# A four-layer graph attention stack on one core: small products on half of the array's columns, edges checked from the 8-bit masks, other durations in the planner

## The chip, the cores and the metric

The kernel runs on one core of a Trainium2 chip. The metric is the device time in microseconds of one execution. Before the change the median of three runs was 3038.52 us (3034.66 to 3041.53). The engines are named as the profile names them: PE (TensorE matmuls), PEld (its weight loads), DVE (VectorE), ACT (ScalarE), POOL (GpSimd) and SP (SyncE, which here only issues transfers).

## The reference, cut to what matters

Sixteen graphs of 1024 nodes with 256 features pass through four attention layers. Every layer normalizes its input, projects it, and adds to it a softmax-weighted sum over the neighbours:

```python
h = jnp.maximum(_layernorm(x, axis=-1), 0.0)
x = x + layer(h, adj)        # four times, each with its own weights
# inside a layer, for every head (4, 4, 4 and 1 heads):
e = leaky_relu(s_src[:, None] + s_dst[None, :], slope)
e = where(adj == 0, -inf, e)
out = softmax(e, axis=-1) @ (h @ W)
```

The adjacency is an int32 matrix of zeros and ones, symmetric here, of 4 MB for each graph. Layer 2 has types of edges in its definition, and after its attention it has a bias, a ReLU, a residual and a normalization over each head.

## The kernel before, in words

Two programs stand in the kernel. `general_path` takes any adjacency; it runs only if a flag `wrong` was set. `fast_path`, which is what the profile shows, assumes edges that are 0 or 1 and values that don't overflow, and checks both while it works: the sums of the edge check land in `sums`, extremes of the softmax totals in `greatest`, and at the end they become `wrong`.

**The main loop.** `fast_path` has 48 units of work in `main`: layers 0 to 2 of 16 graphs, put in an order in which two graphs are under way together. A unit has 4 heads times 8 blocks of 128 source nodes, so 32 tiles, and all units have 1536. A tile goes through three engines. ACT makes `r`, a ReLU over a row of 1024 targets, in one of two wide PSUM buffers (`weigh`). DVE adds a constant, multiplies by the edge mask and writes the numerators `p` to SBUF (`cover`), and with that the wide buffer is free. PE multiplies `p` by the projected features `v` in 16 products of 64 columns by 65 numbers (`gather`): the 128 columns of the array are used as two halves of 64. There are `TILES` = 12 buffers for `p`.

**The preparation of a unit** (`prepare`, with `normal` and `project`). DVE takes statistics (`st`), POOL makes the inverse deviation with a power (`rs<-rs,neg_half`) and normalizes into `hn`, PE transposes `hn` on the full 128 columns, ACT or DVE applies the ReLU (`hT`), PE projects with `wa` on halves of 64 columns, ACT copies to `v`. Then come three small products on PE, once each for a unit, that this change touches. `mx` holds each partition's maxima of the two score vectors; it is transposed (`pp<-ident,mx`), DVE reduces the rows to `top`, and DVE spreads `top` over a small diagonal `diag`. A product of `ones` and `diag` brings the maxima to all partitions (`pp<-diag,ones`). From them DVE and ACT make the exponentials `fac`, and a third product transposes `fac[:, 0]` (`pp<-ident,fac`) to the rows that go to DRAM (`line`) and come back spread over the partitions (`rows`), which `weigh` reads.

**The last layer** has one head. Its numerators are made in halves of 512 (`weigh_some`, `cover`) and multiplied in `last_sums` (`pp<-v_one,p`), spread over later units. `LATE` says how many tiles after its due time its ACT work may fall.

**Masks and edge check.** `load` brings a graph's adjacency as 8-bit numbers to DRAM (`near`, on POOL's queue) and from there transposed to SBUF (`mask`, on SP's queue). `looked_over` reads the same adjacency once more, as int32, in 8 pieces of 512 KB on SP's queue into two buffers `raw`; `look` squares each piece less one half on ACT and writes the sum. The pieces start `LOOK` = 24 tiles after the graph's first unit, and a piece may be fetched only `IDLE` = 6 us after the last but one was looked at.

**The order.** All instructions are put in order ahead of time by a planner. `Plan.cost` gives each instruction a duration and a delay, `Plan.spend` keeps a clock for each engine, and the loop at the end of `fast_path` offers every step that could be next, chooses on every engine the step that is most due among those that could start within `NEAR` = 60 ns of the first, and takes the earliest over the engines. What the planner writes is the fixed order of each engine's queue; on the chip the engines wait for each other by semaphores. All planned instructions are issued from one line of the helper `timed` (L476), so the profile tells them apart by their tiles only.

Of the kernel before, what the change touches and what calls it, by code (L numbers as in the profile page):

```python
# [9 lines left out]
F32 = mybir.dt.float32  # L10
BF16 = mybir.dt.bfloat16
I32 = mybir.dt.int32
I16 = mybir.dt.int16
FP8 = mybir.dt.float8e4
U8 = mybir.dt.uint8
U16 = mybir.dt.uint16
AF = mybir.ActivationFunctionType
# [3 lines left out]
P = 128  # L21
# [347 lines left out]
LEAST = 2.0**-40  # L369
LIVE = 4  # L370
BANKS = 2
TILES = 12
LATE_TILES = 5
LATE = 32
LATE_SUMS = 64
SLACK = 36
FETCH = 15000.0
# [5 lines left out]
LOOK = 24  # L383
IDLE = 6000.0
LANDED = 4000.0
# [22 lines left out]
ACT_LATE = 160.0  # L408
DVE_LATE = 150.0
POOL_LATE = 100.0  # L410
MARK = 20.0


LARGE = ("v_", "x_cur", "mask", "sums", "near", "greatest", "p0", "p1", "p2", "p3", "p4", "p5", "p6", "p7", "p8", "p9", "r_", "po", "pl", "pp", "row", "hT", "raw", "inv")
# [2 lines left out]
class Plan:  # L417
# [19 lines left out]
    def cost(self, engine: str, op: str, a: tuple, k: dict):  # L437
        size = lambda ap: math.prod(ap.shape[1:])
        aps = [v for v in (*a, *k.values()) if hasattr(v, "shape")]
        n = max(size(v) for v in aps)  # L440
        if engine == "PE":
            out, left = a[0], a[1]
            wide = size(left) > 64
            swap = 110.0 if self.mode not in (None, wide) else 0.0
            self.mode = wide
            if op == "transpose":
                return swap + (110.0 if left.dtype == F32 else 56.0), PE_LATE
            if left.dtype != F32:
                return swap + 57.0, PE_LATE
            return swap + max(59.0, size(out) * 0.833 + 3.0), PE_LATE  # L450
        if op == "dma_start":
            total = math.prod(a[0].shape) * mybir.dt.size(a[0].dtype)
            return (600.0 if engine == "POOL" else 60.0), 2200.0 + total / 180.0
        if engine == "ACT":
            return 50.0 + 0.833 * n + (93.0 if "accum_out" in k else 114.0 * sum(size(v) == 1 for v in aps)), ACT_LATE
        if engine == "DVE":
            if op == "reciprocal":
                return 205.0, DVE_LATE
            if op in ("bn_stats", "scalar_tensor_tensor") or n > 64:
                return 70.0 + 1.042 * n + 55.0 * sum(size(v) == 1 for v in aps) + (MARK if n == 512 else 0.0), DVE_LATE  # L460
            return 65.0 + n, DVE_LATE
        if op == "scalar_tensor_tensor":
            return 200.0 + 2.1 * n, POOL_LATE
        if op == "tensor_tensor" and k.get("op", a[-1]) == ALU.pow:
            return 1025.0, POOL_LATE
        return 200.0 + (1.4 if op == "tensor_scalar" else 2.07) * n, POOL_LATE

    def engine(self, eng, name: str):
        plan = self
# [28 lines left out]
def fast_path(  # L498
# [21 lines left out]
    nc = tc.nc  # L520
    ctx.enter_context(tc.manual_schedule())
    plan = Plan()
    pe, act, dve, pool, sp = (
        plan.engine(e, name)
        for e, name in (
            (nc.tensor, "PE"),
            (nc.scalar, "ACT"),
            (nc.vector, "DVE"),
            (nc.gpsimd, "POOL"),
            (nc.sync, "SP"),  # L530
        )
    )
    G, N, F = x.shape
    H, T, HO = a_src_2.shape
    NB = N // P
    KC = F // P
    QUAD = 4
    NQ2 = NB // 2
# [6 lines left out]
    MAXN = max(HEADS)  # L545

    const = ctx.enter_context(tc.tile_pool(name="const", bufs=1))
    ident = const.tile([P, P], F32, name="ident")
    make_identity(nc, ident)
    neg_half = const.tile([P, NB], F32, name="neg_half")  # L550
    nc.vector.memset(neg_half, -0.5)
    ones = const.tile([2 * MAXN, P], F32, name="ones")
    nc.vector.memset(ones, 1.0)

    greatest = const.tile([P, 2, G * LAYERS], F32, name="greatest")

    sums = const.tile([P, G * NB], F32, name="sums")
# [12 lines left out]
    work = ctx.enter_context(tc.tile_pool(name="work", bufs=2))  # L570
    small = ctx.enter_context(tc.tile_pool(name="small", bufs=4))
# [132 lines left out]

    def looked_over(g: "Graph"):

        of = adj[g.b].rearrange("(p r) m -> p (r m)", p=P)
        for k in range(0, N * N // P, N):
            yield "SP", lambda: at_tile[0] >= min(g.until + LOOK, len(tiles)) and (len(looks) < 2 or (looks[-2] is not None and looks[-2] + IDLE))
            raw = work.tile([P, N], I32, name="raw", bufs=2)  # L710
            sp.dma_start(raw, of[:, k : k + N])
            looks.append(None)
            add(g.until + 2 * STEPS, look(raw, len(looks) - 1), plan.now + LANDED)

    def look(raw: bass.AP, k: int):
        yield "ACT", None
        act.activation(raw, raw, AF.Square, bias=-0.5, accum_out=sums[:, k : k + 1])
        looks[k] = plan.now

    looks = []  # L720

    def mask(g: "Graph", j: int):

# [69 lines left out]
    def prepare(u: "Unit"):  # L793

        n, w, layer = u.n, u.w, u.layer
# [12 lines left out]
        v = u.v[:, :, :width].rearrange("p b (h e) -> p b h e", h=n)  # L808
# [20 lines left out]
        for pair in range(NB // 2):  # L829
# [9 lines left out]
            e = Unit()  # L839
            e.u, e.pair, e.turned, e.left = u, pair, False, 2  # L840
            pairs.append(e)
            g = normal(e, rs)
# [1 line left out]

        yield "DVE", lambda: not u.left and u.there
        s, d = (v[:, :, :, w + c].rearrange("p b h -> p h b") for c in range(2))
        mx = small.tile([P, 2, MAXN], F32, name="mx", bufs=3)[:, :, :n]
        dve.tensor_reduce(mx, v[:, :, :, w : w + 2].rearrange("p b h c -> p c h b"), AX.X, ALU.max)
        yield "PE", free_bank
        pm, k = bank()  # L850
        pe.transpose(pm[: 2 * n, :P], mx.rearrange("p c h -> p (c h)"), ident)
        yield "DVE", None
        top = small.tile([2 * MAXN, 1], F32, name="top", bufs=3)
        dve.tensor_reduce(top[: 2 * n], pm[: 2 * n, :P], AX.X, ALU.max)
        drop(k)
        diag = small.tile([2 * MAXN, 2 * MAXN], F32, name="diag", bufs=3)
        dve.tensor_scalar(diag[: 2 * n, : 2 * n], ident[: 2 * n, : 2 * n], top[: 2 * n], None, ALU.mult)
        yield "PE", free_bank
        pa, k = bank()
        pe.matmul(pa[:, : 2 * n], ones[: 2 * n, :], diag[: 2 * n, : 2 * n])  # L860
        yield "DVE", None
        c = small.tile([P, 7, MAXN], F32, name="c", bufs=2)
        S, D, t, c1, c2, b1, b3 = (c[:, i, :n] for i in range(7))
        dve.tensor_copy(c[:, 0:2, :n], pa[:, : 2 * n].rearrange("p (c h) -> p c h", c=2))
        drop(k)
        wide = lambda ap: ap.unsqueeze(2).to_broadcast([P, n, NB])
        arg = small.tile([P, 3, MAXN, NB], F32, name="arg", bufs=3)[:, :, :n, :]
# [30 lines left out]

        add(u.until, others(), plan.now)
        yield "ACT", None  # L900
        act.activation(u.fac[:, 0], arg[:, 0], AF.Exp)
        u.inv = small.tile([P, n, NB], F32, name=f"inv{n}", bufs=3)
        direct = u is main[0] or n == 1 and u.g.b >= G - DIRECT
        if direct:

            yield "PE", free_wide
            pr, k = wide_bank()
            for b in range(NB):
                pe.matmul(pr[:, b * P : (b + 1) * P], u.fac[:, 0, 0, b : b + 1].to_broadcast([P, P]), ident)
            yield "DVE", None  # L910
            over = units.tile([P, N], F32, name="rows", bufs=ROWS)
            dve.tensor_copy(over, pr)
            leave_wide(k)
            u.row.append((over, plan.now))
            if n == 1:
                add(u.until + LATE, last_layer(u), plan.now)
                return
        yield "PE", free_bank
        pr, k = bank()
        pe.transpose(pr[: n * NB, :P], u.fac[:, 0].rearrange("p h b -> p (h b)"), ident)  # L920
        yield "DVE", None
        row = small.tile([MAXN * NB, P], F32, name="row", bufs=1)
        dve.tensor_copy(row[: n * NB], pr[: n * NB, :P])
# [106 lines left out]
    at_tile = [0]  # L1030
# [222 lines left out]
    for b in range(G):  # L1253
        g = Graph()
# [3 lines left out]
        for layer in range(LAYERS):  # L1258
            u = Unit()
# [7 lines left out]
    fresh, live, third = list(layers), [], -3  # L1267
    while fresh or live:
        t = len(main)
        can = [e for e in live if t - e[1] >= 2] or (live if not fresh or len(live) == 2 else [])  # L1270
        pick = None
        for e in can:
            if e[0] == 2 and (t - third >= 3 or not fresh):
                pick = e
        if pick is None:
            pick = max((e for e in can if e[0] < 2), key=lambda e: e[0], default=None)
        if pick is None and fresh and len(live) < 2:
            pick = [0, t, fresh.pop(0)]
            live.append(pick)
        if pick is None:  # L1280
            pick = min(live, key=lambda e: e[1])
        if pick[0] == 2:
            third = t
        main.append(pick[2][pick[0]])
        pick[:2] = [pick[0] + 1, t]
        live = [e for e in live if e[0] < 3]

    if G > 5:

        b = G - 4  # L1290
# [3 lines left out]
    STEPS = H * NB  # L1294
    turn = {(u.g.b, u.layer): k * STEPS for k, u in enumerate(main)}
    begins = []
    for b, us in enumerate(layers):
        us[0].g.until = turn[b, 0] - LOADED
        begins.append((turn[b, 0] - EARLY, load(us[0].g), us[0].g.until))
        for k, u in enumerate(us):  # L1300

            u.past = us[k - 1] if k else None
            if u.n > 1:
                at = turn[b, k] // STEPS
# [20 lines left out]
    def add(until, gen, ready, first=None):  # L1325
        jobs.append([until, ready, *(first or next(gen))[:2], gen])

    tiles = [(u, h, j) for u in main for h in range(H) for j in range(NB)]
    while True:
# [3 lines left out]
        can = []  # L1333
# [9 lines left out]
        if at_tile[0] < len(tiles) and r_ready is not False:  # L1343
            u, h, j = tiles[at_tile[0]]
# [3 lines left out]
        if whole[0] < WHOLES and sum(t is not None for t in p_free) > SPARE:  # L1348
            k = next(
                (  # L1350
                    k
                    for k in range(at_tile[0] + LEAD, min(at_tile[0] + LEAD + NB, len(tiles)))
                    if k not in ahead and tiles[k][2] < NB - LAST
                ),
                None,
            )
            if k is not None:
                u, h, j = tiles[k]
# [10 lines left out]
        for job in jobs:  # L1369
            ready = job[3] is None or job[3]()  # L1370
            if ready:
                ready = max(job[1], ready)
                engine = job[2]
# [7 lines left out]
        for e in ("SP", "POOL", "DVE", "ACT", "PE"):  # L1381
            mine = [c for c in can if c[2] == e]
# [87 lines left out]
```

## Time and profile before

| | before |
|---|---|
| median of three runs | 3038.52 us |
| profiled execution, time | 3040.28 us |
| profiled execution, span | 3038.4 us |
| mean granted TensorE clock | 0.975 |
| PE / PEld busy | 2747.2 / 2257.4 us |
| DVE busy | 2649.5 us |
| ACT busy | 2420.4 us |
| POOL busy | 1572.1 us |
| bytes moved by DMA | 254.02 MB |

The span runs from the first to the last instruction; the profiled execution's time is 1.9 us longer, which is what lies around the span. "Busy" is time in which at least one instruction of an engine is under way. Matmuls overlap each other and their ends are modelled, so PE's busy time is more than what the array needs. A group row of the page gives busy time and the mean duration of one instruction, and then the idle time of its engine just before these instructions with what ended most of it. PE has two records for each fp32 product, so 24,576 products of a `po` tile are 49,152 records.

### The profile page before, as it was taken

What the parts mean: (1) busy time and instruction counts of PE and PEld (TensorE: products, weight loads), DVE (VectorE), ACT (ScalarE), POOL (GpSimd) and SP (SyncE); (2) the same over time, 40 slices, a digit from 0 to 9 for tenths busy, and PEclk for the clock granted to TensorE, in tenths of its full rate; (3) what the DMA queues carried; (4) which work ended last, traced back from release to release, by engine and by line L of the source; (5) the groups of instructions that cost most, each with busy time, mean ns of one, the idle gap of its engine ahead of it and who ended that gap; (6) DMA issues with size and microseconds to landing.
All of it is one profiled execution on the core that took longest, in us unless ns stands there. A gap on an engine that the chain in (4) does not pass through costs nothing.

```text
span 3038.4 us, 129952 instructions
## 1 busy us (share of the span) xinstructions
PE 2747.2 (90%) x58660; PEld 2257.4 (74%) x58660; DVE 2649.5 (87%) x4062; ACT 2420.4 (80%) x3201; POOL 1572.1 (52%) x2263
## 2 busy tenths in 40 slices
PE   6888999899999999899999999999999899989867
PEld 5777777777787777777777777777777777777745
DVE  6889998898989889888988889989898898899973
ACT  5887889778788797878878788787888888888651
POOL 3445673544746547265564646647265473373540
PEclk8999999999999999999999999999999999999979
DMA  8613413325142332414234142422414233311100
GB/s 152 159 68 77 116 38 92 95 67 125 47 109 80 78 106 67 115 61 96 91 73 117 44 102 90 89 92 70 107 68 94 81 84 102 119 43 49 41 8 30
DMA packets 162725, 254.02 MB, mean 84 GB/s; under 512 B 82808, under 2 KB 118384, under 8 KB 161136
## 3 DMA queue, kind: packets, MB, share of 16 engines
q1 hardware_dynamic: 160112, 228.83, 25.3%
q0 software_dynamic: 2048, 16.78, 5.5%
q8 instruction: 462, 7.57, 1.0%
q14 instruction: 103, 0.84, 0.1%
HBM read 261.49 MB, written 34.40 MB: 97 GB/s over the span
## 4 chain that ended last, share of the span: by engine, by line
PE 42%; DVE 27%; ACT 20%; issue 5%; POOL 5%; DMA 0%; ACTq 0%; SPq 0%; DVEq 0%; POOLq 0%
PE pp L476 21%; PE po L476 20%; DVE p L476 17%; ACT r L476 15%; DVE st L476 3%; POOL rs L476 2%; DVE att L476 2%; ACT hT L476 1%; ACT att L476 1%; ACT raw L476 1%; ACT v L476 1%; POOL hn L476 1%; POOL att L476 1%; DVE s L476 1%; DVE c L476 1%
## 5 line engine op out<-in xcount | busy, mean ns | idle before, releaser
L476 ACT ACTIVATE r<-rows,fac 128x1024 f32<-128x1024 f32 (+1 forms) x1552 | 1772.2, 1152 | 349.5 <-DVE p L476 327.1
L476 PE MATMUL po<-v,p 128*64 128x65 f32 x49216 | 1680.7, 226 | 186.3 <-DVE p L476 100.2
L476 PEld LDWEIGHTS po<-v,p 128*64 128x64 f32 x49216 | 1592.9, 140 | 338.1 <-DVE p L476 135.2
L476 DVE SCALAR_TENSOR_TENSOR p<-r,mask 128x1024 f32<-128x1024 f32 x1024 | 1221.7, 1217 | 136.3 <-ACT r L476 112.6
L476 DVE SCALAR_TENSOR_TENSOR p<-r,fac,mask 128x1024 f32<-128x1024 f32 (+1 forms) x768 | 819.4, 1099 | 80.5 <-ACT r L476 71.7
L476 PE MATMUL pp<-wa,hT 128*64 128x264 f32 (+1 forms) x4056 | 520.0, 390 | 21.9 <-ACT hT L476 15.6
L476 POOL TENSOR_TENSOR att<-att,inv 128x512 f32<-128x512 f32 x128 | 133.8, 1045 | 714.1 <-DVE inv L476 576.7
L476 PE MATMUL pp<-v_one,p 128*64 128x257 f32 x3584 | 442.7, 385 | 0.8 <-DVE p L476 0.4
L476 PEld LDWEIGHTS pp<-wa,hT 128*64 128x64 f32 x4056 | 263.2, 138 | 154.3 <-ACT hT L476 25.1
L476 PEld LDWEIGHTS pp<-v_one,p 128*64 128x64 f32 x3584 | 250.3, 139 | 101.4 <-issue 4.4
L476 POOL TENSOR_SCALAR hn<-x_cur,rs 128x256 f32<-128x256 f32 x512 | 283.7, 567 | 44.7 <-PE pp L476 34.6
L476 PE MATMUL pp<-ident,hn 128*128 128x128 f32 x1020 | 182.6, 299 | 57.3 <-POOL hn L476 43.6
L476 POOL TENSOR_TENSOR x_cur<-att,x_cur 128x512 f32<-128x512 f32 x190 | 225.9, 1189 | 14.9
L476 ACT ACTIVATE r<-rows_one,fac 128x512 f32<-128x512 f32 x240 | 185.7, 782 | 20.0 <-DVE p L476 9.6
L476 PEld LDWEIGHTS pp<-ident,hn 128*128 128x128 f32 x1020 | 111.0, 146 | 118.1 <-POOL hn L476 82.4
L476 ACT ACTIVATE hT<-pp 128x512 f32<-128x512 f32 x255 | 150.7, 597 | 42.9 <-PE pp L476 41.2
L476 DVE BATCH_NORM_STATS2 st<-x_cur 128x6 f32<-128x256 f32 x512 | 179.5, 412 | 3.5 <-DMA x_cur<-in_x_dram 3.3
L476 ACT COPY v<-pp 128x264 f32<-128x264 f32 (+1 forms) x395 | 147.2, 386 | 37.4 <-PE pp L476 36.5
L476 POOL TENSOR_TENSOR v<-v,fac 128x512 f32<-128x512 f32 x128 | 137.8, 1097 | 42.4 <-ACT fac L476 42.4
L476 ACT ACTIVATE raw<-raw 128x1024 int32<-128x1024 int32 x128 | 135.0, 1058 | 0.6 <-DMA raw<-in_adj_dram 0.6
L476 POOL TENSOR_TENSOR att<-att,s 128x512 f32<-128x512 f32 x124 | 129.5, 1044 | 10.0
L476 POOL TENSOR_TENSOR rs<-st 128x8 f32<-128x8 f32 x192 | 38.6, 215 | 176.1 <-DVE st L476 174.3
(91 smaller groups left out, 1592.2 us busy)
## 6 DMA issues: line engine op xcount, KB each, us to landing
rows<-line SPq DMA_DIRECT2D x191, 512.0 KB
raw<-in_adj_dram SPq DMA_DIRECT2D x128, 512.0 KB
x_cur<-in_x_dram SPq DMA_DIRECT2D x32, 512.0 KB
near<-in_adj_dram POOLq DMA_DIRECT2D x64, 256.0 KB, 9.0
out_dram<-y SPq DMA_DIRECT2D x128, 128.0 KB
rows_one<-line SPq DMA_DIRECT2D x15, 512.0 KB
mask<-near SPq DMA_TRANSPOSE x64
wa<-in_L_gnn_W_dram SPq DMA_DIRECT2D x6, 128.0 KB
```

What stands on the lines that cost most here:

```text
L476: r = call(*a, **k)
```

## The change

Five things change.

1. The three small products become ordinary products on 64 columns. The inputs lie in one of three zeroed tiles `wide`, with 64 columns for the exponentials, 64 for `mx`, and 8 for `diag`. The transposes become products with the identity, the product with `ones` becomes two, one for each half of the output partitions. The direct route of a few units still uses 128 columns.
2. `looked_over` no longer fetches the adjacency a second time. It reads the 8-bit mask tile of the graph, 8 pieces of 1024 numbers, on ACT, as soon as the masks are loaded, without spacing.
3. `Plan.cost` gets other durations, among them 1650 in place of 1025 ns for POOL's power, 400 in place of 60 ns for an SP transfer, and 1041 in place of 996 ns for a look.
4. `TILES` goes from 12 to 13.
5. `LATE` goes from 32 to 48. `LANES` names a constant that was written as 2 and stays 2.

```diff
-TILES = 12
+TILES = 13
-LATE = 32
+LATE = 48
...
-            return (600.0 if engine == "POOL" else 60.0), 2200.0 + total / 180.0
+            return (600.0 if engine == "POOL" else 400.0), 2200.0 + total / 180.0
+        given = sum(size(v) == 1 for v in aps)
         if engine == "ACT":
-            return 50.0 + 0.833 * n + (93.0 if "accum_out" in k else 114.0 * sum(size(v) == 1 for v in aps)), ACT_LATE
+            if n == 1024:
+                return (1041.0 if "accum_out" in k else (903.0, 1050.0, 1143.0)[given]), ACT_LATE
+            if n <= 64:
+                return 100.0 + 0.7 * n, ACT_LATE
+            return 50.0 + 0.833 * n + 114.0 * given + (40.0 if given == 2 else 0.0), ACT_LATE
...
         if op == "tensor_tensor" and k.get("op", a[-1]) == ALU.pow:
-            return 1025.0, POOL_LATE
-        return 200.0 + (1.4 if op == "tensor_scalar" else 2.07) * n, POOL_LATE
+            return 1650.0, POOL_LATE
+        if op == "tensor_scalar":
+            return (205.0 + 1.3 * n if n > 64 else 270.0), POOL_LATE
+        if n <= 16:
+            return 165.0, POOL_LATE
+        return (1110.0 if n == 512 else 200.0 + 2.07 * n if n > 512 else 200.0 + n), POOL_LATE
...
-    ones = const.tile([2 * MAXN, P], F32, name="ones")
+    ones = const.tile([P, P // 2], F32, name="ones")
     nc.vector.memset(ones, 1.0)
+    wide_of = [const.tile([P, 2 * P // 2 + 2 * MAXN], F32, name=f"wide{k}") for k in range(3)]
+    for t in wide_of:
+        nc.vector.memset(t, 0.0)
...
     def looked_over(g: "Graph"):
-        of = adj[g.b].rearrange("(p r) m -> p (r m)", p=P)
-        for k in range(0, N * N // P, N):
-            yield "SP", lambda: at_tile[0] >= min(g.until + LOOK, len(tiles)) and (len(looks) < 2 or (looks[-2] is not None and looks[-2] + IDLE))
-            raw = work.tile([P, N], I32, name="raw", bufs=2)
-            sp.dma_start(raw, of[:, k : k + N])
-            looks.append(None)
-            add(g.until + 2 * STEPS, look(raw, len(looks) - 1), plan.now + LANDED)
-
-    def look(raw: bass.AP, k: int):
-        yield "ACT", None
-        act.activation(raw, raw, AF.Square, bias=-0.5, accum_out=sums[:, k : k + 1])
+        e = g.edges.bitcast(FP8)
+        for k in range(2 * NQ2):
+            yield "ACT", lambda: max(g.loaded, 1.0)
+            seen = work.tile([P, N], BF16, name="seen", bufs=1)
+            at = g.b * NB + k
+            of = e[:, k // 2, (k % 2) * N : (k % 2 + 1) * N]
+            act.activation(seen, of, AF.Square, bias=-0.5, accum_out=sums[:, at : at + 1])
...
-        mx = small.tile([P, 2, MAXN], F32, name="mx", bufs=3)[:, :, :n]
+        mine = wide_of[turns_of[0] % len(wide_of)]
+        turns_of[0] += 1
+        diag = mine[:, P:]
+        mine = mine[:, :P].rearrange("p (c m) -> p c m", c=2)
+        mx = mine[:, 1, : 2 * n].rearrange("p (c h) -> p c h", c=2)
...
-        pe.transpose(pm[: 2 * n, :P], mx.rearrange("p c h -> p (c h)"), ident)
+        pe.matmul(pm[: P // 2, :P], mine[:, 1, :], ident)
...
-        diag = small.tile([2 * MAXN, 2 * MAXN], F32, name="diag", bufs=3)
...
-        pe.matmul(pa[:, : 2 * n], ones[: 2 * n, :], diag[: 2 * n, : 2 * n])
+        for half in range(0, P, P // 2):
+            pe.matmul(pa[half : half + P // 2, : 2 * n], ones, diag[:, : 2 * n])
...
-        act.activation(u.fac[:, 0], arg[:, 0], AF.Exp)
+        near_end = mine[:, 0, : n * NB].rearrange("p (h b) -> p h b", h=n)
+        act.activation(near_end, arg[:, 0], AF.Exp)
...
-        pe.transpose(pr[: n * NB, :P], u.fac[:, 0].rearrange("p h b -> p (h b)"), ident)
+        pe.matmul(pr[: P // 2, :P], mine[:, 0, :], ident)
```

More of the change, by code (lines that the diff above doesn't have):

```diff
@@ L410 @@
 POOL_LATE = 100.0
-MARK = 20.0
+LANES = 2
 LARGE = ("v_", "x_cur", "mask", "sums", "near", "greatest", "p0", "p1", "p2", "p3", "p4", "p5", "p6", "p7", "p8", "p9", "r_", "po", "pl", "pp", "row", "hT", "raw", "inv")
@@ L452, in cost @@
             total = math.prod(a[0].shape) * mybir.dt.size(a[0].dtype)
-            return (600.0 if engine == "POOL" else 60.0), 2200.0 + total / 180.0
+            return (600.0 if engine == "POOL" else 400.0), 2200.0 + total / 180.0
+        given = sum(size(v) == 1 for v in aps)
         if engine == "ACT":
-            return 50.0 + 0.833 * n + (93.0 if "accum_out" in k else 114.0 * sum(size(v) == 1 for v in aps)), ACT_LATE
+            if n == 1024:
[3 more added lines that the diff above has]
+            return 50.0 + 0.833 * n + 114.0 * given + (40.0 if given == 2 else 0.0), ACT_LATE
         if engine == "DVE":
             if op == "reciprocal":
[L458 to L463, printed above, removed]
-        if op == "tensor_tensor" and k.get("op", a[-1]) == ALU.pow:
-            return 1025.0, POOL_LATE
-        return 200.0 + (1.4 if op == "tensor_scalar" else 2.07) * n, POOL_LATE
+                return 200.0, DVE_LATE
+            if op == "bn_stats":
+                return 327.0, DVE_LATE
+            if op == "scalar_tensor_tensor" and n == 512 and not given:
+                return 716.0, DVE_LATE
+            if op == "scalar_tensor_tensor" and n > 64 or n > 64:
+                return 73.0 + 1.042 * n + 52.0 * given, DVE_LATE
+            return 90.0 + n, DVE_LATE
+        if op == "tensor_tensor" and k.get("op", a[-1]) == ALU.pow:
+            return 1650.0, POOL_LATE
[4 more added lines that the diff above has]
+        return (1110.0 if n == 512 else 200.0 + 2.07 * n if n > 512 else 200.0 + n), POOL_LATE
     def engine(self, eng, name: str):
@@ L551, in fast_path @@
     nc.vector.memset(neg_half, -0.5)
-    ones = const.tile([2 * MAXN, P], F32, name="ones")
+    ones = const.tile([P, P // 2], F32, name="ones")
     nc.vector.memset(ones, 1.0)
+    wide_of = [const.tile([P, 2 * P // 2 + 2 * MAXN], F32, name=f"wide{k}") for k in range(3)]
+    for t in wide_of:
+        nc.vector.memset(t, 0.0)
+    turns_of = [0]
     greatest = const.tile([P, 2, G * LAYERS], F32, name="greatest")
@@ L705, in looked_over @@
     def looked_over(g: "Graph"):
-        of = adj[g.b].rearrange("(p r) m -> p (r m)", p=P)
-        for k in range(0, N * N // P, N):
-            yield "SP", lambda: at_tile[0] >= min(g.until + LOOK, len(tiles)) and (len(looks) < 2 or (looks[-2] is not None and looks[-2] + IDLE))
-            raw = work.tile([P, N], I32, name="raw", bufs=2)
-            sp.dma_start(raw, of[:, k : k + N])
-            looks.append(None)
-            add(g.until + 2 * STEPS, look(raw, len(looks) - 1), plan.now + LANDED)
-    def look(raw: bass.AP, k: int):
-        yield "ACT", None
-        act.activation(raw, raw, AF.Square, bias=-0.5, accum_out=sums[:, k : k + 1])
-        looks[k] = plan.now
-    looks = []
+        e = g.edges.bitcast(FP8)
[5 more added lines that the diff above has]
+            act.activation(seen, of, AF.Square, bias=-0.5, accum_out=sums[:, at : at + 1])
     def mask(g: "Graph", j: int):
@@ L908, in prepare @@
             for b in range(NB):
-                pe.matmul(pr[:, b * P : (b + 1) * P], u.fac[:, 0, 0, b : b + 1].to_broadcast([P, P]), ident)
+                pe.matmul(pr[:, b * P : (b + 1) * P], near_end[:, 0, b : b + 1].to_broadcast([P, P]), ident)
             yield "DVE", None
@@ L1269, in fast_path @@
         t = len(main)
-        can = [e for e in live if t - e[1] >= 2] or (live if not fresh or len(live) == 2 else [])
+        can = [e for e in live if t - e[1] >= LANES] or (live if not fresh or len(live) == LANES else [])
         pick = None
@@ L1276, in fast_path @@
             pick = max((e for e in can if e[0] < 2), key=lambda e: e[0], default=None)
-        if pick is None and fresh and len(live) < 2:
+        if pick is None and fresh and len(live) < LANES:
             pick = [0, t, fresh.pop(0)]
```

## The prediction, made before the changed kernel ran

> **What bounds the kernel now.** I read the page from the top: busy shares, then the chain of work that ended last, then the groups of instructions.
>
> ```profile
> PE 2747.2 (90%) x58660; PEld 2257.4 (74%) x58660; DVE 2649.5 (87%) x4062; ACT 2420.4 (80%) x3201; POOL 1572.1 (52%) x2263
> PE 42%; DVE 27%; ACT 20%; issue 5%; POOL 5%; DMA 0%; ACTq 0%; SPq 0%; DVEq 0%; POOLq 0%
> PE pp L476 21%; PE po L476 20%; DVE p L476 17%; ACT r L476 15%; DVE st L476 3%; POOL rs L476 2%; DVE att L476 2%; ACT hT L476 1%; ACT att L476 1%; ACT raw L476 1%; ACT v L476 1%; POOL hn L476 1%; POOL att L476 1%; DVE s L476 1%; DVE c L476 1%
> L476 ACT ACTIVATE r<-rows,fac 128x1024 f32<-128x1024 f32 (+1 forms) x1552 | 1772.2, 1152 | 349.5 <-DVE p L476 327.1
> L476 DVE SCALAR_TENSOR_TENSOR p<-r,mask 128x1024 f32<-128x1024 f32 x1024 | 1221.7, 1217 | 136.3 <-ACT r L476 112.6
> ```
>
> No engine is full and no transfer is on the chain. PE, DVE and ACT hand it to each other, PE holding most: 42% of the span. A microsecond taken from PE is worth between 0.42 (only where PE was on the chain) and 1 (if the planner's order follows PE everywhere).
>
> The waits say what the two wide buffers do: ACT waits for DVE to free one, DVE for ACT to fill one, and PE for `hn`.
>
> ```profile
> ACT r L476 <- DVE p L476: 336.7, 477, 6.2
> DVE p L476 <- ACT r L476: 184.2, 306, 4.0
> PE pp L476 <- POOL hn L476: 43.6, 26, 16.3
> ```
>
> **What the Trainium skill says.** "TensorEngine Tiling (Array Packing)", Key Properties: changing the tiling mode, not just the tile, drains the engine; its Restrictions rule out fp32 transpose mode with column tiling, which is why the change multiplies by the identity. "TensorE: Matmul & The Clock Gate", part 3, adds that products on different column groups run side by side. Both agree with the timeline of PE. These are one transposition of `mx`, one product with `diag` and one transposition of `fac`, each on 128 columns inside a run of `po` on 64:
>
> ```profile
> 1259.79 1.40 PE L476 MATMUL po<-v,p 128*64 128x65 f32 x42
> 1261.12 0.27 PE L476 MATMUL pp<-ident,mx 128*8 128x128 f32 x1
> 1261.32 2.09 PE L476 MATMUL po<-v,p 128*64 128x65 f32 x64
> 1263.34 0.38 PE L476 MATMUL pp<-diag,ones 8*128 8x8 f32 x2
> 1263.65 0.97 PE L476 MATMUL po<-v,p 128*64 128x65 f32 x21
> ...
> 1317.78 1.75 PE L476 MATMUL po<-v,p 128*64 128x65 f32 x54
> 1319.46 0.28 PE L476 MATMUL pp<-ident,fac 128*32 128x128 f32 x1
> 1319.67 1.04 PE L476 MATMUL po<-v,p 128*64 128x65 f32 x28
> ```
>
> Another stretch gives the undisturbed pace:
>
> ```profile
> 1004.25 3.65 PE L476 MATMUL pp<-v_one,p 128*64 128x257 f32 x32
> 1007.73 6.70 PE L476 MATMUL po<-v,p 128*64 128x65 f32 x224
> ```
>
> A record of `po` takes 6.70/224 = 29.9 ns. So 42 records fill 1.26 of the 1.53 us from 1259.79 to 1261.32, and `mx` took the other 0.27; in the same way `diag` took 2.33 - 64 x 0.0299 = 0.42 and `fac` 1.89 - 54 x 0.0299 = 0.28. These are prices with the switch to the other mode and back.
>
> "ScalarE: Activation LUTs", What ACT_TABLE_LOAD costs, gives an activation one element a cycle, fp32 and bf16 alike. The trace agrees for int32: looks follow each other at 0.95 us plus 0.09 for the read of the sum. No run here shows 8-bit input.
>
> **The change part by part.**
>
> *Small products.* In the order of the two programs PE changes between 64 and 128 columns 775 times before and 399 times after; what stays are the transpositions of `hn`. A unit's three products cost 0.27 + 0.42 + 0.28 = 0.97 us. After: in the row of `v_one`, 32 records take 3.48 us, so two products side by side (4 records) 435 ns for 257 columns. A product alone keeps its half that long: 128 columns 435 x 128/257 = 217 ns, twice in a unit. The two products with `diag` have 8 columns and no row like them; I take the price of a pair of `po`, 120 ns. Together 0.55 us, saving 0.41 us, in 64 preparations (48 units and 16 last layers) 26 us of PE. Ends: 40 if the lone product runs wholly beside its neighbours, 10 if it holds up both halves. On the chain this is worth 26 x 0.42 = 11 to 26 us; I take 17.
>
> *Power priced 1650 instead of 1025 ns.* The row by form says the new price is the chip's:
>
> ```profile
> L476 POOL TENSOR_TENSOR rs<-rs,neg_half 128x8 f32<-128x8 f32 x64 | 106.0, 1657 | 5.0
> ```
>
> In 64 preparations the planner was 0.63 us early, 40 us in all, close to the 43.6 us PE stands still for `hn`, with tile products queued behind the transpositions and everybody behind those. With the right price other products go first. Worth 0 to 44; I take 12, since what is put first can itself be late. The other new prices move single instructions by under 60 ns, except SP's 400 for 60, which makes the planner expect rows 0.3 us later. SP issues only.
>
> *Looks.* 128 looks stay on ACT and cost the same, taken from the int32 row. Their places change. Between tiles the order before has 72 single looks and 28 pairs; after, 102 singles, 7 pairs, 2 triples and, in the first unit, one run of six. During a run DVE has at most one finished `r`, 1.14 us of work (its instructions follow each other so), so a pair (2.08 us) leaves it dry for 0.94, a triple 1.98, six 5.1. Before 28 x 0.94 = 26 us, after 6.6 + 4.0 + 5.1 = 16. Gain 11, on the chain 3 to 11; I take 6. If 8-bit input took twice as long, 122 us more on ACT at its 20% of the chain would be 24 us lost; that goes into the range. `seen` has one buffer, so a look right after another waits out its write, 0.1 us (1.05 long against 0.95 apart), some 26 times at most.
>
> *Transfers.* 128 pieces of 512 KB, 67 MB of 254, and their issues on SP go; `rows`, `line` and `out` no longer queue behind them. Of the waits on ACT hardly any is theirs:
>
> ```profile
> L476 ACT ACTIVATE raw<-raw x128: 1040/1050/1137, 73.8 to 2667.4; 128x1024 int32<-128x1024 int32 x128
> ...
>   DMA raw<-in_adj_dram: 0.6, 1
> ```
>
> The chain in order of time has one stretch of 5.4 us behind such a transfer (at 2539). Worth 0 to 8; I take 2.
>
> *Thirteenth buffer.* DVE waits for PE to free a `p` for 7.1 us in all: 0 to 7, I take 1. *`LATE`.* The last layer's PE products per unit go from runs such as 32, 96, 0 to 16, 64, 48: more even, costed at nothing, -5 to +5. *Three zeroed tiles* are memsets like the one of `ones` (0.17 us) while DVE waits 3.3 us for the first input: nothing.
>
> Sum: 17 + 12 + 6 + 2 + 1 = 38 us. The profiled execution took 3040.3 us (span 3038.4 and 1.9 around it), the median is 1.8 lower: 3038.5 - 38 = about 3001.
>
> **The rivals.**
>
> *No gain.* PE's time is freed, but it only stands longer waiting for `p`, because DVE and ACT keep each other's pace through two buffers (336.7 and 184.2 us). For it: in undisturbed stretches a tile costs DVE 1.14 us and PE 0.96 (32 records). Against: PE holds 42% of the chain. Then only a few microseconds remain: 3035.
>
> *Slower, by looks.* They now start as soon as the masks are there, with no spacing. If the gaps on ACT in which the planner puts them are not there on the chip, each delays `r`, and through it DVE and PE. Now `ACT raw` is 1% of the chain, some 30 us. The sum of gains without looks is 32, so it decides from (30 + 32)/1.04 = 60 of 128 looks on the chain. With 90 there it is 94 - 62 = 32 us slower, 3070. Against: the runs got shorter.
>
> *It doesn't do what it says.* Lone products on half of the columns might drain PE as before, for instance with the full-width `ident` as the other operand. Then 17 of the 38 are lost: 3018.
>
> **How the numbers follow.** Likeliest, as summed: 0.66, own range 2972 to 3028 (the low and the high ends of the parts do not fall together). No drain saved: 0.10, at 3018. No gain: 0.11, at 3035. Slower by looks or by an order that fits worse: 0.13, at 3070. A measurement of this kernel tells 0.2%, 6 us, from no change: faster is below 3032.4, and takes the first two cases and a little of the third, 0.78; same 0.09; slower 0.13. Eight times in ten: 2965 to 3042.
>
> **What would show it.** In the profile after: PE rows `pp<-ident,wide` and `pp<-wide,ones` on 64 columns, no step of 0.15 to 0.2 us at their edges, and PE's busy time down by some 20 us; `PE pp <- POOL hn` below 30 us; `ACT raw` gone and `ACT seen` at most 1% of the chain, 1.04 us each; 187 MB moved. The prediction is wrong if `DVE p <- ACT r` grows by tens of us, or if PE's idle time grows by what its work shrank.

## The result and the profile after

The changed kernel took 3015.2 us (median of four runs, 3013.71 to 3019.46), against 3039.7 us before (with a fourth run added to the three): a ratio of 0.9924, interval 0.9907 to 0.9941, so about 24 us or 0.8% faster. The forecast was 3001 us with a range of 2965 to 3042. The direction and the range held, though the range of 77 us held the kernel before as well; the gain is about two thirds of the 38 us of the sum. The profiled execution took 3014.4 us, its span 3012.4.

First the engines' busy time and the chain that ended last, by engine and by line:

```profile
PE 2694.6 (89%) x58915; PEld 2262.8 (75%) x58915; DVE 2650.3 (88%) x4065; ACT 2414.9 (80%) x3201; POOL 1571.0 (52%) x2263
PE 35%; DVE 29%; ACT 21%; POOL 7%; issue 5%; DMA 1%; SPq 0%; ACTq 0%; POOLq 0%; DVEq 0%
DVE p L487 19%; PE pp L487 19%; PE po L487 16%; ACT r L487 15%; DVE st L487 3%; POOL att L487 2%; ACT seen L487 2%; DVE att L487 2%; ACT att L487 1%; DVE s L487 1%; DVE c L487 1%; POOL rs L487 1%; POOL hn L487 1%; ACT v L487 1%; ACT hT L487 1%
```

PE's busy time is down by 53 us and its share of the chain by seven points, while DVE and ACT do the same work as before and hold a little more of the chain. The span is only 26 us shorter: PE's idle time (span less busy time) went from 291 to 318 us, so half of what its work shrank went into waiting. The prediction had named idle time that grows by as much as the work shrank as a sign of being wrong; half of that came. Then the waits that answer to the three shown before, in us in total, times, and the longest:

```profile
ACT r L487 <- DVE p L487: 349.2, 454, 5.9
DVE p L487 <- ACT r L487: 157.8, 264, 5.7
...
PE pp L487 <- POOL hn L487: 51.8, 32, 15.3
```

DVE waits for ACT 26 us less. PE's wait for `hn`, which was to fall below 30 us, rose from 43.6 to 51.8. The DMA engines moved 186.91 MB, as forecast. The timeline of PE shows what a small product costs now, inside a run of `po`:

```profile
975.98 1.15 PE L487 MATMUL po<-v,p 128*64 128x65 f32 x32
976.98 0.38 PE L487 MATMUL pp<-ident,wide 128*64 128x128 f32 x2
977.11 1.18 PE L487 MATMUL po<-v,p 128*64 128x65 f32 x32
```

```profile
263.23 1.15 PE L487 MATMUL po<-v,p 128*64 128x65 f32 x32 [0.47 <-ACT att L487]
264.22 0.24 PE L487 MATMUL pp<-wide,ones 128*64 128x8 f32 x4
264.31 1.89 PE L487 MATMUL po<-v,p 128*64 128x65 f32 x58
```

At the prediction's pace of 29.9 ns a record, 32 records of `po` fill 0.96 us. From 975.98 to 977.11 are 1.13 us, so the product with `wide` took 0.17; from 263.23 to 264.31 are 1.08, so the two with `ones` took 0.12. That pace is a little high, since it counts the run-out of the last record. The next line of the same stretch shows the 224 records from 1007.73 to 1014.26, which is 29.2 ns each:

```profile
1014.26 3.65 PE L476 MATMUL pp<-v_one,p 128*64 128x257 f32 x32
```

The merged lines also hide that the second pair of `po` after a product on 128 columns still starts 0.05 us late. The starts of the single records give the whole delay that a product hands to the `po` records behind it. The median over all places inside an unbroken run of `po` (40 to 91 of each kind), at 29.2 ns a record, was 0.35 us for `mx`, 0.46 for `diag` and 0.36 for `fac` before, and now 0.19 for each product with `wide` and 0.12 for the two with `ones`. The step from the last `po` to the product is 0.06 us in the stretch at 975.98, where it was 0.15 before, and the one from the product's last record to the next `po` is 0.03, where it was 0.20. "TensorEngine Tiling (Array Packing)" of the Trainium skill calls this drain a property of changing the mode, in Key Properties; the traces put it at 1.18 - 0.49 = 0.69 us for a unit's three products, 44 us for 64 preparations if all stand in such runs. The sum had taken 0.41 and 26.

The looks, by tile, with minimum, median and maximum in ns:

```profile
L487 ACT ACTIVATE seen<-mask x128: 1039/1046/1118, 38.1 to 2561.7; 128x1024 bf16<-128x1024 fp8e4 x128
```

8-bit input costs ACT what int32 did (median 1050), so the cost kept for the range didn't come.

### The profile page after: what moved, and what is told of

It is laid out like the page before. It is cut to its first block, busy times and chain, and to the rows that moved or that the text cites. A ratio compares the mean times of both kernels' runs of the same rounds, so it can differ in the third digit from the quotient of the medians.

```text
span 3012.4 us, 130240 instructions
## 1 busy us (share of the span) xinstructions
PE 2694.6 (89%) x58915; PEld 2262.8 (75%) x58915; DVE 2650.3 (88%) x4065; ACT 2414.9 (80%) x3201; POOL 1571.0 (52%) x2263
## 2 busy tenths in 40 slices
DMA packets 144292, 186.91 MB, mean 62 GB/s; under 512 B 80760, under 2 KB 116336, under 8 KB 142704
## 4 chain that ended last, share of the span: by engine, by line
PE 35%; DVE 29%; ACT 21%; POOL 7%; issue 5%; DMA 1%; SPq 0%; ACTq 0%; POOLq 0%; DVEq 0%
DVE p L487 19%; PE pp L487 19%; PE po L487 16%; ACT r L487 15%; DVE st L487 3%; POOL att L487 2%; ACT seen L487 2%; DVE att L487 2%; ACT att L487 1%; DVE s L487 1%; DVE c L487 1%; POOL rs L487 1%; POOL hn L487 1%; ACT v L487 1%; ACT hT L487 1%
## 5 line engine op out<-in xcount | busy, mean ns | idle before, releaser
L487 PE MATMUL pp<-v_one,p 128*64 128x257 f32 x3584 | 430.7, 383 | 2.7 <-DVE p L487 1.8
L487 PEld LDWEIGHTS pp<-wa,hT 128*64 128x64 f32 x4056 | 269.3, 138 | 138.9 <-ACT hT L487 16.5
L487 PEld LDWEIGHTS pp<-v_one,p 128*64 128x64 f32 x3584 | 267.2, 138 | 95.2 <-DVE p L487 9.0
L487 PE MATMUL pp<-ident,hn 128*128 128x128 f32 x1020 | 178.8, 295 | 63.5 <-POOL hn L487 51.8
L487 ACT ACTIVATE seen<-mask 128x1024 bf16<-128x1024 fp8e4 x128 | 134.6, 1052 | 0.4
```

The source lines that it names most:

```text
L487: r = call(*a, **k)
```

## The experiments

All orders are made ahead, so almost any edit gives another order of all instructions, and the time of one order is in part chance, as the nudges at the end show. I therefore separated what an edit does on the chip from what the new order does. Ratios are to the kernel before, timed beside each kernel. Single executions of one kernel spread over some 6 to 20 us, so medians and intervals count, and a single profiled span does not.

| run | what it is | median us | ratio, interval |
|---|---|---|---|
| e1 | before, looks from masks | 3037.7 | 0.9991 (0.9983 to 1.0000) |
| e2 | e1, products on 64 columns, order of e1 | 3027.8 | 0.9964 (0.9952 to 0.9977) |
| e3 | changed, products on the full array, order kept | 3032.7 | 0.9976 (0.9968 to 0.9984) |
| e4 | changed, old prices | 3011.0 | 0.9909 (0.9894 to 0.9924) |
| e5 | e2, products priced as they are | 3034.1 | 0.9985 (0.9977 to 0.9993) |
| e6 | e5 with TILES 13 (e4 with LATE 32) | 3012.6 | 0.9907 (0.9890 to 0.9924) |
| e7 | changed, LATE 32 | 3015.8 | 0.9923 (0.9909 to 0.9936) |
| e8 | changed, planner nudged by 2 ns | 3035.6 | 0.9988 (0.9980 to 0.9995) |
| e9 | e5's order with 13 buffers | 3030.2 | 0.9973 (0.9961 to 0.9984) |
| e10 | before, nudge that changed no order | 3039.7 | 1.0003 (0.9993 to 1.0012) |
| e11 | changed, another nudge | 3007.2 | 0.9894 (0.9874 to 0.9913) |
| e12 | e4, nudged | 3019.4 | 0.9935 (0.9915 to 0.9955) |

**The looks alone (e1).** `looked_over` of the changed kernel in the kernel before, nothing else.

```diff
-            raw = work.tile([P, N], I32, name="raw", bufs=2)
-            sp.dma_start(raw, of[:, k : k + N])
...
+            of = e[:, k // 2, (k % 2) * N : (k % 2 + 1) * N]
+            act.activation(seen, of, AF.Square, bias=-0.5, accum_out=sums[:, at : at + 1])
```

> The kernel before with one part of the change: the edge check reads the 8-bit masks on ACT as they are loaded, so 128 transfers of 512 KB are gone; products, prices, TILES and LATE as before, and the planner makes a new order of it. Theory of the prediction: looks and transfers are worth 8 us (3 to 21), so about 3032 us. Rival, the transfers carry the change: most of its 24.5 us are here, 3020 us or less. Rival, any new order moves the time by chance: anywhere from 3025 to 3055.

A gain of 0.09%, 2.7 us (0 to 5 by the interval). Leaving out 67 MB of transfers, for which ACT had waited 0.6 us in the trace before, bought next to nothing; the gain that the rival expects is not seen. But e1 is a new order too, a single draw, and its looks are not spread as in the changed kernel: between tiles its trace has 94 single looks, 4 pairs, 4 triples, 2 runs of four and one of six. By the prediction's own count they leave DVE dry for 23 us, against 26 before and 16 in the changed kernel. So e1 does not test the better spread.

**The small products at a fixed order (e2, e3).** In e2 the products are on 64 columns, but the planner is given the old price of each, so all engines' orders are those of e1 except for the products themselves:

```diff
+        plan.priced = (False, 110.0)
-        pe.transpose(pm[: 2 * n, :P], mx.rearrange("p c h -> p (c h)"), ident)
+        pe.matmul(pm[: P // 2, :P], mine[:, 1, :], ident)
...
-        pe.matmul(pa[:, : 2 * n], ones[: 2 * n, :], diag[: 2 * n, : 2 * n])
+        for half in range(0, P, P // 2):
+            plan.priced = (True, 0.0 if half else 59.0)
+            pe.matmul(pa[half : half + P // 2, : 2 * n], ones, diag[:, : 2 * n])
```

> The kernel of e1 with the three small products on 64 columns, but priced by the planner as they were, so that every engine's order is that of e1. What moves is the mode change alone. Theory: 17 us below e1 (11 to 26), PE busy down by some 26 us. Rival, PE only waits longer for p: within 5 us of e1, and PE's wait for DVE p up by some 20 us.

The reverse was done to the changed kernel, again with the order kept:

```diff
+        plan.priced = (False, 109.624)
-        pe.matmul(pm[: P // 2, :P], mine[:, 1, :], ident)
+        pe.transpose(pm[: 2 * n, :P], mine[:, 1, : 2 * n], ident)
...
-        for half in range(0, P, P // 2):
-            pe.matmul(pa[half : half + P // 2, : 2 * n], ones, diag[:, : 2 * n])
+        plan.priced = (False, 118.0)
+        pe.matmul(pa[:, : 2 * n], ones[: 2 * n, :], diag[: 2 * n, : 2 * n])
...
+        plan.priced = (False, 109.624)
-        pe.matmul(pr[: P // 2, :P], mine[:, 0, :], ident)
+        pe.transpose(pr[: n * NB, :P], mine[:, 0, : n * NB], ident)
```

> The changed kernel with the three small products back on the full array (8, 32 and 128 columns, as before), priced as the narrow ones, so that every engine's order is that of the changed kernel. Theory: the mode changes cost 17 us here too (11 to 26), about 3032 us. Rival, PE is no longer what bounds (35% of the chain): under 8 us, 3016 to 3023 us.

By the ratios the narrow products are worth 0.9991 - 0.9964 = 0.0027, 8 us, in the order of e1, and 0.9976 - 0.9924 = 0.0052, 16 us, in that of the changed kernel (9.9 and 17.5 us by the medians). In both pairs the intervals are apart. The order was the same in each pair (the traces show it), and so was the mean granted clock of the runs (0.977 in both, 0.974 in both), so this is what the narrow form of the products does on the chip. The first gain lies below the 11 to 26 us of the theory, the second inside. In the changed order the rival of under 8 us falls; in that of e1 the rival of under 5 us is unlikely but not excluded, since the intervals leave anything from 0.0006 to 0.0048. The longer wait that this rival names is not seen: PE's `po` products waited for `p` as before (105.2 us in e1, 105.8 in e2). In the page of e3 PE holds more of the chain than in the changed kernel:

```profile
PE 44%; DVE 26%; ACT 18%; POOL 6%; issue 5%; DMA 1%; SPq 0%; ACTq 0%; POOLq 0%; DVEq 0%
```

That share is no measure of the drains by itself, since it moves with the order: e8 and e6, with narrow products, show 42% and 43%, e11, the fastest, 40%, and e2 31%. Of PE's time only a part came out at the end. Of the 44 us, which hold if every product stands in an unbroken run, it is 0.19 in the order of e1 and 0.36 in that of the changed kernel; of what PE's busy time differs by in the single profiles (19 us from e1 to e2, 41 from e3 to the changed kernel) it is 0.44 and 0.39.

**The prices (e4, e12).** The changed kernel with the whole of the old `Plan.cost`; the power's price stands for the others here.

```diff
-            return 1650.0, POOL_LATE
+            return 1025.0, POOL_LATE
```

> The changed kernel with the old Plan.cost, all else as changed; the order is made anew. Theory of the prediction: the right price of POOL's power is worth 12 us (0 to 44), so about 3027 us. Rival: since PE's wait for hn did not shrink in the changed kernel (51.8 us after 43.6), the prices are worth nothing by themselves: 3010 to 3020 us. Rival, chance of the order: anywhere from 3000 to 3035 us.

It is not slower: 0.9909 against 0.9924, with intervals that overlap. Two more pairs among the runs below differ in the prices alone: e6 against e7, 0.9907 and 0.9923, and e12, which nudges e4, against e8, 0.9935 and 0.9988. In all three the old prices have the lower ratio, by 5, 5 and 16 us, and only in the last are the intervals apart. The price of the power was not changed by itself in any run.

> The kernel of e4 (all of the change but the prices) with the planner's delay after a PE instruction at 212 instead of 210 ns. Theory, the prices are worth nothing and each order is a draw: 3005 to 3035 us. If orders by the old prices are robust, within 5 of 3011 us; if it is below 3005 it is the best kernel of the study.

**From e2 to e4 in steps (e5, e6, e7).** Between 3027.8 and 3011.0 us lie the products' own price, `TILES` and `LATE`.

e5 is e2 without its lines of given prices:

```diff
-        plan.priced = (False, 110.0)
...
-            plan.priced = (True, 0.0 if half else 59.0)
```

> The kernel of e2 (looks from the masks, products on 64 columns, TILES 12, LATE 32, old prices), but with the products priced as what they are now, so that the planner makes its own order. First of three steps from e2 (3027.8 us) to e4 (3011.0 us). Theory: the planner's order gains from knowing that the array does not change its mode, some 5 us: 3023 us. Rival, TILES and LATE make the step: 3028 us within 4. Rival, chance of the order: anywhere from 3015 to 3040.

e6 is e5 with one buffer more:

```diff
-TILES = 12
+TILES = 13
```

> As e5, with TILES 13 and LATE still 32, which is e4 with LATE 32. Second step. Theory of the prediction: a thirteenth buffer is worth 1 us (0 to 7), so within 4 of e5. Rival, the buffer lets ACT and DVE run ahead of PE, and the 17 us are here: 3011 us within 4.

e7 is the changed kernel with the old `LATE`:

```diff
-LATE = 48
+LATE = 32
```

> The changed kernel with LATE 32, all else as changed. Theory of the prediction: LATE is worth nothing, -5 to 5 us: 3010 to 3020. Rival, the later due time of the last layer spreads PE's work and gives the rest of the gain: 3025 or more.

Each of these steps compares two orders, so it holds the chance of an order too. The own price costs 6 us instead of gaining 5. `LATE` shows nothing, in both places (e7 against the changed kernel, e6 against e4). The step to `TILES` = 13 is 0.9985 to 0.9907, 24 us, by far the largest. e9 asks whether that is the buffer: 13 buffers on the chip, taken in turn, in the order that the planner made for 12.

```diff
+    held, idle = {}, list(range(TILES + 1))
...
-        return probs.tile([P, N], F32, name=f"p{k}"), k
+        held[k] = idle.pop(0)
+        return probs.tile([P, N], F32, name=f"p{held[k]}"), k
...
+            idle.append(held[k])
```

> The kernel of e5 with 13 buffers for p on the chip, but the planner still counting 12, so that every engine's order is that of e5; the next buffer is the one longest free. It tells whether the 21 us between e5 (3034.1) and e6 (3012.6) are the buffer or the order made with it. Theory, the order: 3034 us within 4, since DVE waits for a free p for under 15 us in any trace. Rival, the buffer: 3013 to 3020 us.

0.9985 becomes 0.9973: 4 us (-2 to 10 by the intervals, which overlap). So the smaller part of the 24 us, if any, is the buffer under the old order; the rest came with the order made for 13 buffers. DVE's wait for PE to free a `p` did not shrink either: 4.9 us in e5, 8.2 in e9, 12.3 in e6. (It was 21.2 us in e4, over the 15 us that the expectation gives for any trace.) The order made for 13 was not run on 12 buffers.

**Nudges (e8, e10, e11).** A planner's delay moved by 2 ns means nothing to the chip, and the work stays the same to the last instruction.

In e8, e10 and e12 it is the first of these lines, in e11 the second.

```diff
-PE_LATE = 210.0
+PE_LATE = 212.0
...
-DVE_LATE = 150.0
+DVE_LATE = 152.0
```

> The changed kernel with the planner's delay after a PE instruction at 212 instead of 210 ns, a change without meaning on the chip that only makes another order. It measures what an order is worth by chance. If orders of one quality differ little, 3015 us within 4; if the steps of e1 to e7 are partly chance, some 8 us or more away, either side.

> The changed kernel with the planner's delay after a DVE instruction at 152 instead of 150 ns: a third order of the changed work, beside 3015.2 and the 3035.6 of e8. Theory, e8 was an unlucky transient in the first 640 tiles and not the level: 3010 to 3030. Rival, the changed kernel's own order is the lucky one and 3035 the level: 3030 to 3040.

> The kernel before with the planner's delay after a PE instruction at 212 instead of 210 ns, nothing else: another order of the same work. Theory, orders of the same work lie up to 20 us apart: more than 6 us away from 3039, on either side. Rival, only the changed kernel's order was a lucky one: 3039 us within 6.

e10 failed as an experiment: the nudge left the order of every engine as it was. It serves as a control, and its 1.0003 says how well two measurements of one order agree. How far nudged orders of the kernel before would lie apart stays unknown. e8 and e11 did change the order, and the same work took 3035.6 and 3007.2 us: one nudge gave back nearly the whole gain, the other added 8 us to it and fell below both of its forecasts. With e12 against e4 (3019.4 and 3011.0) there are three pairs of nudged orders, 8, 8 and 20 us apart.

Where they part is seen by counting tiles. The order of e8 parts from that of the changed kernel 0.33 ms into the span, the one of e11 at 0.76 ms. These rows count the ACT instructions that read `rows` in two stages of equal length for each kernel (start and end of the stage, its length, busy time of ACT with the count, granted clock, DMA). First the changed kernel, then e8, then e11:

```profile
480.00:1200.00 720.00, 0.00 (x0) 429.69 (x378) 0.99 0.26 64
1200.00:2540.00 1340.00, 0.00 (x0) 808.66 (x710) 0.99 0.27 66
```

```profile
480.00:1200.00 720.00, 0.00 (x0) 416.04 (x364) 0.97 0.26 63
1200.00:2540.00 1340.00, 0.00 (x0) 811.48 (x713) 0.98 0.27 65
```

```profile
480.00:1200.00 720.00, 0.00 (x0) 445.38 (x391) 0.99 0.26 65
1200.00:2540.00 1340.00, 0.00 (x0) 798.96 (x701) 0.99 0.27 65
```

In the first 480 us they made 256, 256 and 254 tiles. So at 1200 us the changed kernel has 634, e8 620 and e11 645; at 720/378 = 1.9 us each e8 is 27 us behind and e11 21 ahead. At 2540 us they have 1344, 1333 and 1346. The lag of e8 arises in that one stretch and stays: the 700th and the 1500th `r` that read `rows` start 27 and 28 us later than in the changed kernel. The lead of e11 does not stay: it is 35 us at the 1200th and 5 at the 1500th, so tiles made early don't tell what e11 gains in the end. Which instructions do it was not found: the waits of the stretch differ by a few us in many places.

Part of it goes with the granted clock, which the rows show as 0.97 for e8 in that stretch and 0.99 for the other two. The runs of the changed kernel had 0.974 in the mean, those of e8 0.970 and those of e11 0.976. Among the runs of one and the same kernel, those with 0.001 less clock were 1.4 us longer (one slope for all kernels on record). By that estimate the clock goes with 6 of the 20 us of e8 and 3 of the 8 us of e11, but with nothing between e4 and e12, which had the same. Why an order gets another clock was not looked into.

## Why the prediction was right, point by point

The forecast was right in direction and range; its time was 14 us too low. The parts came out less well than the whole. Only the small products are shown at a fixed order; the other terms were 21 us together, and what the runs have in their place is mostly one large step with the order for 13 buffers. That the sum came near is in part luck.

*Small products: right in mechanism, with two sizes wrong that made up for each other.* The gain is shown at a fixed order twice: 17 us taken of 11 to 26, measured 8 and 16. The time taken from PE was forecast at 26 us, with ends of 10 and 40, and is 44 by the single records. The wide products had been counted too cheap (0.97 us a unit for 1.18), because of the pace and of the late second pair behind each; a product alone on its half was estimated at 0.22 us and took 0.19, the pair with `ones` at 0.12 and took 0.12. The weight was too high: the prediction put it "between 0.42 (only where PE was on the chain) and 1" and took 17/26 = 0.65, and the runs give 0.19 to 0.44. Part of the freed time went into waiting: PE's idle time grew by 27 us over the whole change.

*Price of the power: wrong, 12 us taken, none found.* The reading that failed is that the planner's 40 us were "close to the 43.6 us PE stands still for `hn`". Two waits, at the two ends of the span, make up 32 of those 43.6 us:

```profile
16.35 2.09 PE L476 MATMUL pp<-ident,hn 128*128 128x128 f32 x7 [16.35 <-POOL hn L476]
...
2941.91 2.31 PE L476 MATMUL pp<-ident,hn 128*128 128x128 f32 x8 [15.72 <-POOL hn L476]
```

The other 24 waits, each under 1 us, are 11.5 us in all, and only these have the size of an error of 0.63 us. With the right price these waits, without the two at the ends, rose to 26 us, and with the old one in e4 the kernel was no slower. "The other new prices move single instructions by under 60 ns" does not hold either: by the two versions of `Plan.cost`, POOL's operations on 512 numbers (818 of them) went from 1260 to 1110 ns. What each price does alone was not tested.

*Looks and transfers: 8 us taken, 2.7 measured in e1, where the looks are spread otherwise.* In the changed kernel the runs of looks got shorter as counted, but `ACT seen` holds 2% of the chain where `ACT raw` held 1%; the forecast was at most 1%. The rival "slower, by looks" points at this, but e1 was not slower. What the spread of the changed kernel is worth was not measured by itself.

*Thirteenth buffer: right on the chip as far as e9 can tell, mis-sized as a part of the change.* 1 us taken of 0 to 7; 4 at a fixed order. The order that the planner makes with it brought 20 us more in e6, and that term was not in the sum.

*`LATE`: nothing forecast, nothing seen.* *The other rivals* ("no gain", "it doesn't do what it says") fall with the timelines and e3, though "no gain" describes half of what PE gave up.

What was left out is the size of chance. "An order that fits worse" stood only as a mishap inside one rival at 0.13, while nudged orders of the same work lie up to 28 us apart. The changed kernel's 3015 us are one draw: seven orders with the narrow products and 13 buffers (the changed kernel, e4, e6, e7, e8, e11, e12) run from 3007 to 3036 us. All lie below the kernel before, and six of them more than 8 us below e2, so the change as a whole is faster than that kernel, itself one draw; how much of what 13 buffers gave beyond 4 us is a better rule and how much luck stays open. The steps of the ladder are looks 3, products 8, own price -6, `TILES` with its order 24, `LATE` -1 and prices -5, together 23 us; that they add up says nothing, since each is a difference between neighbours, and only the products are apart from the order.

The fastest kernel of the study by its median is e11, ratio 0.9894 (0.9874 to 0.9913), 8 us below the changed one by a nudge alone; the intervals of e4 and e6 overlap with its.

## What to carry to other kernels

A small product on the full array between products on 64 columns held up those behind it by 0.35 to 0.46 us here, with 8 columns as with 32, and one in their mode by 0.12 to 0.19 us; put small products in the mode of their neighbours even if half of the array stands empty. Don't count the time taken from an engine as gained: here PE held 0.37 to 0.44 of the chain, and 0.19 to 0.44 of what it gave up reached the end. Where a program is ordered ahead by a planner, compare an edit at a fixed order, and nudge the planner by something without meaning before believing a gain of under one per cent. A waiting time that equals an error of the planner is no evidence that mending the error removes the wait; look first where the single waits lie.

## What the runs showed that I had not expected

The same instructions in two orders took 3007.2 and 3035.6 us, 0.9% apart, after a change of 2 ns in a planner's delay. The mean granted clock differed between orders of the same work, 0.970 to 0.976. In the kernel before, a transposition with 8 stationary columns held up narrow products by 0.35 us, about as much as one with 32 (0.36), while the steps at the edges of products laid out on 64 columns are gone: a product that fills fewer columns is not for that in the narrow mode. And ACT took 1.046 us for 1024 numbers of 8 bits, as for int32.
